# Second layer of a graph network: 15 block products of 512 columns in place of 7 products of 384, with sums moved between engines

## The chip, the cores and the metric

The kernel runs on one core of one Trainium2 chip. The core has a matrix engine (TensorE, PE in the profile, its weight loads shown as PEld), a vector engine (VectorE, DVE), a scalar engine (ScalarE, ACT), a general engine (GpSimd, POOL) and SyncE (SP), which here only issues transfers. Each works through its own list of instructions in order, and they wait for each other by semaphores. The metric is the device time of one execution in microseconds.

## The reference

Two layers run over 128 graphs of 64 nodes with 768 features, so over 8192 rows. In each layer the rows are normalised and clipped at zero (h), and the layer's result is added to its input. The change leaves the first layer's mathematics alone. The second is:

```python
h = jnp.maximum(_layernorm(x, axis=-1), 0.0)
# for each of 6 heads (768 -> 128 columns): hh = h @ W
attn = tanh(hh) @ w_src + swapaxes(tanh(hh) @ w_dst, -1, -2)
attn = softmax(where(adj == 0, -999, leaky_relu(attn, 0.2)))
feat = elu(attn @ hh + b)
gate = sigmoid(h @ H_w.T + H_b)
x = x + gate * feat + (1.0 - gate) * h
```

The heavy part is h times two 768x768 matrices: the six heads side by side (`w_cat`) and the gate (`hw_t`). Everything is float32.

## The kernel before, in words

A tile is 128 rows, that is two graphs; a pair p is two tiles, t0 = 2p and t1 = 2p + 1, and there are 32 pairs. The program has two passes over all pairs.

The first pass (from L289) computes layer 0. Each pair needs 15 block products of a 2x3 by 3x3 scheme, with three weights one after the other in each product (L549, 90 matmuls of 256 columns). `A_SUMS` and `B_SUMS` (L23, L37) are the sums of operand blocks and weight blocks, and `PRODUCTS` (L54) lists each product's operands, its PSUM bank, whether it starts the bank anew, and the output block its bank is added to. `finish` (L571) normalises the pair's result, and stores h in `H1D` and x + h in `XH1`, both in device memory. During the last pair `fetch` (L270) loads and combines the second layer's weights.

The second pass (from L641) computes layer 1. For each pair, `turn` (L704) transposes h through PSUM and makes the operands of a Winograd form of the 2x2 by 2x2 scheme: seven products p1 to p7 (L774 on), each of three matmuls of 384 columns, once for the heads (s = 0) and once for the gate (s = 1). That makes 42 matmuls per pair (L738), in six PSUM banks: three names with two buffers each. `copy` and `add` (L755, L769) take the banks into the tiles HS (heads) and Z (gate).

Then each tile goes through a chain of small steps:
- `heads` (L811): tanh on ScalarE (L814); the product with w_src on GpSimd (L816), summed per head on ScalarE with six accumulating copies (L824); the product with w_dst summed by VectorE (L821); six small GpSimd steps (L825 to L832) split the sums into three bf16 parts.
- `rows` (L840): a matmul turns the sums into rows, which VectorE (L846) and ScalarE (L848) lay out.
- `softmax` (L854): a matmul gives the logits (L860); VectorE keeps those of edges (L862), ScalarE applies the leaky slope (L864), VectorE takes the maximum (L866), ScalarE six exponentials with their sums (L870), VectorE divides (L872, L873).
- `turn_p` and `attend` (L877, L888): transposes of the probabilities and 24 matmuls of 64 rows; VectorE adds the bias (L903). `swap` (L834) fetches the rows of the other graph by a transfer inside the core.
- `final` (L905): an exponential on ScalarE (L911) and four VectorE operations over 768 columns (L912 to L915), then a plain transfer to the output (L916).

The order is written as steps: `main(p)` gives a list of matmul steps, and `merged` (L176) places the side steps of `before` (the next pair's operands) and `behind` (the previous pair's chain) at given step numbers. The build then fixes one list per engine, in which nothing overtakes.

Of the kernel before, what the change touches and what calls it, by code (L numbers as in the profile page):

```python
# [8 lines left out]
F32 = mybir.dt.float32  # L9
# [61 lines left out]

PLACES = ("g6", "g10", "b11", "b21", "g12", "w", "g14", "b01", "b10", "b20", "b02", "b12", "b22",
          "v", "b00")


@with_exitstack
def kernel(
# [24 lines left out]

# [58 lines left out]
    XH1 = [dram.tile([2 * P, D], F32, name=f"xh1_{p}") for p in range(NP)]  # L166
# [30 lines left out]
    nc.vector.memset(mhalf, -0.5)  # L197

# [33 lines left out]

    PL = 3 * KQ * CQ
    BL = KH * HALF
# [5 lines left out]
    def signed(to, s0, x, s1, y):  # L240

        if s0 == "-":
# [4 lines left out]
    NAMES2 = ("11", "21", "T3", "22", "T1", "T2", "T4")  # L247
    bv = {n: [of_weights((2 * i + s) * BL, BL).rearrange("p (k n) -> p k n", k=KH) for s in range(2)]
          for i, n in enumerate(NAMES2)}
    REST = 2 * len(NAMES2) * BL  # L250
    rest = [of_weights(REST + i * D, D) for i in range(9)]
    assert REST + 9 * D <= len(PLACES) * PL

    SUMS2 = {"T1": ("T3", "11"), "T2": ("22", "T1"), "T4": ("21", "T2"), "T3": ("22", "T3")}

    def sum_of_weights(to):
        a, b = SUMS2[to]
        for s, t in enumerate(bv[to]):
            nc.vector.tensor_sub(t, bv[a][s], bv[b][s])
# [10 lines left out]
    def fetch():  # L270

        def blk_of(name, h, q):
            for s, src in enumerate((w_cat, hw_t)):
                nc.sync.dma_start(
                    bv[name][s],
                    src[h * HALF : (h + 1) * HALF, q * HALF : (q + 1) * HALF].rearrange(
                        "(k p) n -> p k n", p=P))

        return [(30, lambda: load_h(0)),
                (13, lambda: blk_of("11", 0, 0)),  # L280
                (20, lambda: blk_of("21", 1, 0)),
                (31, lambda: blk_of("T3", 0, 1)),
                (37, lambda: blk_of("22", 1, 1)),
                (52, lambda: (sum_of_weights("T1"), sum_of_weights("T3"))),
                (57, lambda: sum_of_weights("T2")),
                (68, lambda: sum_of_weights("T4"))]


    with ExitStack() as px:  # L289
# [29 lines left out]
        bw = {n: of_weights(i * PL, PL) for i, n in enumerate(PLACES)}  # L319

# [7 lines left out]
        def form_b(n):  # L328

            s0, x, s1, y, at = B_SUMS[n]  # L330
            if at:
                bw[n] = bw[at]
            tc.keep_in_program_order(signed(bw[n], s0, bw[x], s1, bw[y]))
# [237 lines left out]
        def finish(p):  # L571
            for k in range(2):
                t = 2 * p + k
                to = small.tile([P, 2], F32, name="rn")
                stats(X[t], to)
                h = keep.tile([P, D], F32, name="hf", bufs=2)
                nc.scalar.activation(h, X[t], AF.Relu, scale=to[:, 0:1], bias=to[:, 1:2])
                nc.sync.dma_start(H1D[p][k * P : (k + 1) * P, :], h)
                nc.gpsimd.tensor_add(X[t], X[t], h)
                nc.sync.dma_start(XH1[p][k * P : (k + 1) * P, :], X[t])  # L580
# [60 lines left out]
    with ExitStack() as px:  # L641
# [5 lines left out]
        XH, AI = {}, {}  # L647
# [10 lines left out]
        def load_x(p):  # L658
            for k in range(2):
                t = 2 * p + k  # L660
                XH[t] = work.tile([P, D], F32, name="x", bufs=3)
                nc.sync.dma_start(XH[t], XH1[p][k * P : (k + 1) * P, :])
# [4 lines left out]
        hbb = rest[6]  # L667
        wsd = wb.tile([P, 2, D], F32, name="wsd")
        nc.sync.dma_start(bb, row(b_att, P))
        nc.sync.dma_start(hbb, row(hb, P))  # L670
# [30 lines left out]
        HS, HX, Z, PB = {}, {}, {}, {}  # L701
        A11, A12, A22, S1, S2, S3, S4 = {}, {}, {}, {}, {}, {}, {}

        def turn(p, k, h):  # L704

            ps = pss.tile([P, KH, P], F32, name="ps")
            for i in range(KH):
                kb = h * KH + i
                nc.tensor.transpose(ps[:, i, :], H1[2 * p + k][:, kb * P : (kb + 1) * P], ident)  # L709

            def new(which, name):
                which[p] = work.tile([P, KH, P], F32, name=name)
                return which[p]

            if (k, h) == (0, 0):
                nc.scalar.copy(new(A11, "a11"), ps)
            elif (k, h) == (0, 1):
                nc.scalar.copy(new(A12, "a12"), ps)
            elif (k, h) == (1, 1):
                nc.scalar.copy(new(A22, "a22"), ps)  # L720
            else:
                nc.vector.tensor_sub(new(S3, "s3"), A11[p], ps)
                nc.vector.tensor_add(new(S1, "s1"), A22[p], ps)  # L723
                nc.gpsimd.tensor_sub(new(S2, "s2"), S1[p], A11[p])
                nc.gpsimd.tensor_sub(new(S4, "s4"), A12[p], S2[p])

        def main(p):

            bank = {}
            steps = []  # L730
            t0, t1 = 2 * p, 2 * p + 1

            def mm(b, s, a, w, first):
                for q in range(KH):
                    def step(q=q):
                        if first and q == 0:
                            bank[b, s] = psm.tile([P, 512], F32, name="pm" + ("c" if b == "d" else b))
                        nc.tensor.matmul(bank[b, s][:, :HALF], a[p][:, q, :], bv[w][s][:, q, :],  # L738
                                         start=(first and q == 0), stop=(q == KH - 1),
                                         skip_group_check=True)  # L740
                    steps.append(step)

            def after(step):
                last = steps[-1]
                steps[-1] = lambda: (last(), step())

            def part(t, s, q):
                if s == 0:
                    return HS[t][:, q * HH : (q + 1) * HH, :]
                return Z[t][:, q * HALF : (q + 1) * HALF].rearrange("p (h o) -> p h o", h=HH)  # L750

            def sums(b, s):
                return bank[b, s][:, :HALF].rearrange("p (h o) -> p h o", h=HH)

            def copy(t, s, q, b):  # L755
                def step():
                    if t not in HS:
                        HS[t] = rest[t % 4].rearrange("p (h o) -> p h o", h=H)
                    if s == 1 and t not in Z:
                        Z[t] = work.tile([P, D], F32, name="z", bufs=4)  # L760
                    if s == 0:
                        nc.scalar.copy(part(t, s, q), sums(b, s))
                    else:
                        nc.vector.tensor_add(  # L764
                            part(t, s, q), sums(b, s),
                            hbb[:, q * HALF : (q + 1) * HALF].rearrange("p (h o) -> p h o", h=HH))
                after(step)

            def add(t, s, q, b):  # L769
                def step():  # L770
                    nc.vector.tensor_add(part(t, s, q), sums(b, s), part(t, s, q))
                after(step)

            def p1(s):  # L774
                mm("a", s, A11, "11", True)
                copy(t0, s, 0, "a")

            def p2(s):
                mm("c", s, A12, "21", True)
                add(t0, s, 0, "c")  # L780

            def p5(s):
                mm("b", s, S1, "T1", True)
                copy(t1, s, 1, "b")

            def p6(s):
                mm("a", s, S2, "T2", False)
                copy(t0, s, 1, "a")

            def p4(s):  # L790
                mm("d", s, A22, "T4", True)
                copy(t1, s, 0, "d")

            def p7(s):
                mm("a", s, S3, "T3", False)
                add(t1, s, 0, "a")
                add(t1, s, 1, "a")

            def p3(s):
                mm("b", s, S4, "22", False)  # L800
                add(t0, s, 1, "b")

            order = ((p1, 0), (p2, 0), (p5, 0), (p1, 1), (p6, 0), (p2, 1), (p5, 1), (p4, 0),
                     (p6, 1), (p7, 0), (p4, 1), (p3, 0), (p7, 1), (p3, 1))
            if p == NP - 1:
                order = [(f, s) for s in range(2) for f in (p1, p2, p5, p6, p4, p7, p3)]
            for f, s in order:
                f(s)
            return steps

        def heads(t):  # L811
# [3 lines left out]
            pr = work.tile([P, H, DO], F32, name="pr", bufs=1)  # L815
            nc.gpsimd.tensor_mul(pr, th, wsd[:, 0, :].rearrange("p (h o) -> p h o", h=H))  # L816
            sd = small.tile([P, H], F32, name="sd")
            sg = small.tile([P, 3, H], F32, name="sg")
            for h in range(H):
                no = work.tile([P, DO], F32, name="no", bufs=1)  # L820
# [206 lines left out]
```

## Time and profile before

The time is 2554.71 us, the median of three runs (2554.43 to 2555.62). The profiled execution spans 2552.4 us, with a mean granted TensorE clock of 0.993.

| engine | busy, us | share of the span | instructions |
|---|---|---|---|
| PE | 2501.2 | 98% | 12780 |
| PEld | 1858.1 | 73% | 12780 |
| DVE | 1977.2 | 77% | 4309 |
| ACT | 887.8 | 35% | 2596 |
| POOL | 566.0 | 22% | 863 |

The first pass ends at about 1514 us, where the first transposes of the second pass stand in the time line. A row of the page gives each engine's busy share in 40 slices of 64 us, in tenths (9 is 90% or more). A time line's row gives start, length, engine, line, operation, output<-inputs, shapes, count, and in brackets how long the engine was idle before it and what ended that. A window's row gives the window, its length, and then busy time and count for PE, PEld, DVE, ACT and POOL, the granted clock, the share of the transfer engines and GB/s. Register, branch and semaphore instructions are not counted as busy.

### The profile page before, as it was taken

Reading aid. Unit: us, or ns where it says so; the run is one execution under the profiler, and the core shown is the slowest. Engines: PE = TensorE matmul, PEld = TensorE weight load, DVE = VectorE, ACT = ScalarE, POOL = GpSimd, SP = SyncE. Lnnn points to the kernel's source line nnn. Section 1 sums busy time; section 2 is a strip of 40 time slices with the busy share of each in tenths; the row PEclk is TensorE's granted clock in tenths of the full one; section 3 lists DMA queues with packets and bytes.
Section 4 is the critical chain, followed back from the end, with each engine's and each line's share of the span. In section 5 each row is a group of like instructions: output and inputs, shape, how many; then the busy total and the mean of one; then the engine's idle time right before and its main releaser. Section 6 shows DMA issues by size and latency. Waiting matters only on the chain.

```text
span 2552.4 us, 35949 instructions
## 1 busy us (share of the span) xinstructions
PE 2501.2 (98%) x12780; PEld 1858.1 (73%) x12780; DVE 1977.2 (77%) x4309; ACT 887.8 (35%) x2596; POOL 566.0 (22%) x863
## 2 busy tenths in 40 slices
PE   5999999999999999999999999999999999999996
PEld 4888888888888888888888875656556665656663
DVE  8977677776777777777777446888888888888888
ACT  1221211212212112121121215555555555555555
POOL 0111121111211112111111023333333333333332
PEclk8999999999999999999999999999999999999998
DMA  5112121121111211112111152333333333333332
GB/s 174 44 52 67 40 78 41 41 78 40 67 52 40 79 40 58 60 40 79 40 48 67 38 190 64 102 102 102 102 102 102 102 102 101 102 102 102 101 101 81
DMA packets 104134, 199.06 MB, mean 78 GB/s; under 512 B 35354, under 2 KB 46221, under 8 KB 103954
## 3 DMA queue, kind: packets, MB, share of 16 engines
q1 hardware_dynamic: 103800, 196.70, 24.2%
q8 instruction: 101, 1.65, 0.3%
q14 instruction: 79, 0.65, 0.1%
q10 hardware_dynamic: 154, 0.06, 0.0%
HBM read 95.67 MB, written 75.50 MB: 67 GB/s over the span
## 4 chain that ended last, share of the span: by engine, by line
PE 92%; DVE 3%; DMA 2%; issue 1%; POOL 1%; ACT 1%; SPq 0%; DVEq 0%; POOLq 0%; ACTq 0%
PE pwa L549 19%; PE pwb L549 16%; PE pma L738 14%; PE pmb L738 10%; PE pmc L738 9%; PE pwc L549 6%; PE pwd L549 6%; PE pb L502 5%; PE ps L898 2%; PE ps L709 2%; PE ps L882 1%; PE pwd L533 1%; DVE op L245 1%; DVE weights L245 0%; DMA weights<-in_wself_t_dram 0%
## 5 line engine op out<-in xcount | busy, mean ns | idle before, releaser
L549 PE MATMUL pwa<-weights,op 128*128 128x256 f32 x2304 | 542.8, 383 | 4.1 <-DVE x L541 2.9
L549 PEld LDWEIGHTS pwa<-weights,op 128*128 128x128 f32 x2304 | 423.3, 190 | 73.3 <-DVE x L541 11.7
L510 ACT COPY op<-pb 128x768 f32<-128x768 f32 x160 | 124.1, 797 | 841.4 <-PE pb L502 841.4
L549 PE MATMUL pwb<-weights,op 128*128 128x256 f32 x1536 | 372.5, 383 | 12.6 <-DVE x L543 9.5
L245 DVE TENSOR_TENSOR op<-op 128x768 f32<-128x768 f32 x256 | 238.7, 953 | 154.2 <-ACT op L510 154.1
L549 PEld LDWEIGHTS pwb<-weights,op 128*128 128x128 f32 x1536 | 285.8, 191 | 60.8 <-DVE x L543 10.7
L738 PE MATMUL pmb<-weights,s 128*128 128x384 f32 x768 | 295.1, 494 | 0.5 <-DVE s L723 0.5
L738 PE MATMUL pmc<-weights,a 128*128 128x384 f32 x768 | 285.4, 488 | 0.0
L738 PE MATMUL pma<-weights,s 128*128 128x384 f32 x768 | 279.4, 486 | 0.0
L481 POOL COPY c<-cnt 128x243 bf16<-128x243 bf16 x64 | 46.3, 751 | 721.4 <-PE pb L489 674.3
L738 PEld LDWEIGHTS pmb<-weights,s 128*128 128x128 f32 x768 | 137.6, 190 | 87.1 <-issue 17.3
L738 PEld LDWEIGHTS pma<-weights,s 128*128 128x128 f32 x768 | 140.0, 190 | 80.8 <-DVE z L764 0.2
L738 PEld LDWEIGHTS pmc<-weights,a 128*128 128x128 f32 x768 | 136.5, 190 | 81.9 <-issue 12.3
L816 POOL TENSOR_TENSOR pr<-th,wsd 128x768 f32<-128x768 f32 x64 | 119.5, 1868 | 299.6 <-ACT th L814 236.4
L549 PE MATMUL pwc<-weights,op 128*128 128x256 f32 x768 | 184.9, 383 | 0.0
L219 DVE BATCH_NORM_STATS2 st<-x 128x6 f32<-128x384 f32 x256 | 138.3, 552 | 50.2 <-DMA x<-in_x_dram 48.8
L549 PE MATMUL pwd<-weights,op 128*128 128x256 f32 x768 | 176.2, 379 | 0.0
L226 POOL TENSOR_TENSOR rn<-ve,mhalf 128x1 f32<-128x1 f32 x128 | 70.8, 553 | 470.0 <-DVE ve L225 466.4
L549 PEld LDWEIGHTS pwc<-weights,op 128*128 128x128 f32 x768 | 143.2, 190 | 25.1 <-issue 7.0
L502 PE MATMUL pb<-r,h 64*128 64x192 f32 x1536 | 153.0, 340 | 8.0 <-ACT h L411 7.7
L549 PEld LDWEIGHTS pwd<-weights,op 128*128 128x128 f32 x768 | 145.9, 190 | 19.8
L502 PEld LDWEIGHTS pb<-r,h 64*128 64x128 f32 x1536 | 124.7, 189 | 42.8 <-issue 30.5
(150 smaller groups left out, 3944.4 us busy)
## 6 DMA issues: line engine op xcount, KB each, us to landing
x<-in_x_dram SPq DMA_DIRECT2D x64, 384.0 KB
h<-hf SPq DMA_DIRECT2D x64, 384.0 KB
xh<-x SPq DMA_DIRECT2D x64, 384.0 KB
h<-h SPq DMA_DIRECT2D x64, 384.0 KB
x<-xh SPq DMA_DIRECT2D x64, 384.0 KB
weights<-weights SPq DMA_DIRECT2D x128, 192.0 KB
out_dram<-f SPq DMA_DIRECT2D x62, 384.0 KB
ai<-in_adj_dram SPq DMA_DIRECT2D x64, 64.0 KB
```

The source lines that it names most:

```text
L219: ins = nc.vector.bn_stats(st[:, i, :], src[:, i * HALF : (i + 1) * HALF])
L226: nc.gpsimd.tensor_tensor(to[:, 0:1], ve, mhalf, op=OP.pow)
L245: return (nc.vector.tensor_add if s1 == "+" else nc.vector.tensor_sub)(to, x, y)
L481: nc.gpsimd.tensor_copy(c3, CNT[p][:, k, :, None].to_broadcast([P, NROW, 3]))
L502: nc.tensor.matmul(ps[:, g, i * 3 * N : (i + 1) * 3 * N], H0[t][s, kb * P : (kb + 1) * P], rts[p % 2][s, k].rearrange("p s n -> p (s n)"), ...
L510: nc.scalar.copy(a.rearrange("p h s (g n) -> p g (h s) n", g=GT), ps[:, :, : 6 * N].rearrange("p g (x n) -> p g x n", n=N))
L533: nc.tensor.matmul(bank[b][:, :CQ], CT_T[p, k][: 3 * (e - a), i, :], tabs[i][:, q * CQ : (q + 1) * CQ], start=(first and i == 0), stop=Tru ...
L549: nc.tensor.matmul(bank[b][:, :CQ], OPS[p, an][:, q, s, :], bw[bn][:, (s * KQ + q) * CQ : (s * KQ + q + 1) * CQ], start=(first and q == s ...
L709: nc.tensor.transpose(ps[:, i, :], H1[2 * p + k][:, kb * P : (kb + 1) * P], ident)
L738: nc.tensor.matmul(bank[b, s][:, :HALF], a[p][:, q, :], bv[w][s][:, q, :], start=(first and q == 0), stop=(q == KH - 1), skip_group_check= ...
L816: nc.gpsimd.tensor_mul(pr, th, wsd[:, 0, :].rearrange("p (h o) -> p h o", h=H))
L898: nc.tensor.matmul(po[r][o, c, :], PT[t][s, c, o], (HS if r == g else HX)[t][s, 2 * c + r, :], start=True, stop=True)
```

## The change

The second pass takes over the first pass's 2x3 by 3x3 scheme. h is cut in blocks of 128 rows by 256 columns, each weight in blocks of 256 by 256. The two weights' blocks stand side by side, so that one matmul has 512 columns, the first 256 for the heads and the others for the gate. A product is two such matmuls, and a pair has 15 products, 30 matmuls. For the last pair the products are done for the heads first and then for the gate, with 256 columns. PSUM: two buffers for bank a, one for each of b, c and d, two for everything else.

What moves beside it:
- the operand sums (`form`) are 11 VectorE operations of 256 columns per pair, in place of two VectorE and two GpSimd sums of 384;
- the first addition into an output block is split: ScalarE copies the heads' half, VectorE adds the gate's bias to the other;
- `heads`: one VectorE product of 1536 columns for both w_src and w_dst, and twelve accumulating copies on ScalarE;
- the division of the softmax moves behind the attention: six VectorE operations of 128 columns multiply by the reciprocal sum and add the bias;
- `finish` stores (h + 1)/2 in `HHD` (one more ScalarE operation and transfer), and x + h directly in the output; `final` then needs three VectorE operations, and adds its result to the output by an accumulating transfer issued by GpSimd;
- `heads` of tile t0 starts in the tile's own pair, at step 25 of 30, instead of the next.

The purpose is fewer matmul columns per pair on TensorE, with less work for VectorE and GpSimd around them. The core of the diff:

```diff
 def finish(p):   # first pass
-                nc.sync.dma_start(XH1[p][k * P : (k + 1) * P, :], X[t])
+                nc.sync.dma_start(of[t * P : (t + 1) * P, :], X[t])
+                hh = keep.tile([P, D], F32, name="hh", bufs=1)
+                nc.scalar.activation(hh, h, AF.Identity, scale=0.5, bias=half)
+                nc.sync.dma_start(HHD[p][k * P : (k + 1) * P, :], hh)
...
+        def form(p, *names):
+            for n in names:
+                s0, x, s1, y = A_SUMS[n]
+                t = OPS[p, n] = work.tile([P, KQ, P], F32, name="op", bufs=17)
+                signed(t, s0, OPS[p, x], s1, OPS[p, y])
...
+            def read(b, c, sign, first, ss):
+                k, q = int(c[0]), int(c[1])
+                cols = slice(q * CQ, (q + 1) * CQ)
+                to = hzs[(2 * p + k) % 4][:, ss, cols]
+                ps = bank[b][:, : (ss.stop - ss.start) * CQ].rearrange("p (s n) -> p s n", n=CQ)
+                op = nc.vector.tensor_add if sign == "+" else nc.vector.tensor_sub
+                if not first:
+                    if sign == "+":
+                        op(to, ps, to)
                     else:
+                        op(to, to, ps)
+                    return
+                if ss.start == 0:
+                    nc.scalar.activation(to[:, 0], ps[:, 0], AF.Copy,
+                                         scale=1.0 if sign == "+" else -1.0)
...
+            def product(an, bn, b, first, c, sign, begins, ss):
+                def step(q):
+                    if first and q == 0:
+                        bank[b] = psm.tile([P, 512], F32, name=f"pm{b}", bufs=2 if b == "a" else 1)
+                    n = ss.stop - ss.start
+                    nc.tensor.matmul(
+                        bank[b][:, : n * CQ], OPS[p, an][:, q, :],
+                        bw2[bn][:, (2 * q + ss.start) * CQ : (2 * q + ss.stop) * CQ],
+                        start=(first and q == 0), stop=(q == KQ - 1), skip_group_check=True)
+                    if q == KQ - 1:
+                        read(b, c, sign, begins, ss)
...
 def heads(t):
-            nc.gpsimd.tensor_mul(pr, th, wsd[:, 0, :].rearrange("p (h o) -> p h o", h=H))
+            nc.vector.tensor_mul(pr, th[:, None].to_broadcast([P, 2, H, DO]),
+                                 wsd.rearrange("p s (h o) -> p s h o", h=H))
...
             for h in range(H):
-                nc.vector.scalar_tensor_tensor(no, th[:, h, :], 1.0, wsd[:, 1, h * DO : (h + 1) * DO],
-                                               op0=OP.mult, op1=OP.mult, accum_out=sd[:, h : h + 1])
+                nc.scalar.activation(pr[:, 1, h, :], pr[:, 1, h, :], AF.Copy, accum_out=sd[:, 1, h : h + 1])
...
 def attend(t):
-            for r in range(2):
-                nc.vector.tensor_add(fv[:, r], po[r], bb[:, None, :].to_broadcast([P, HH, DO]))
+            for h in range(H):
+                nc.vector.scalar_tensor_tensor(
+                    FF[t][:, h * DO : (h + 1) * DO], po[h % 2][:, h // 2, :], DN[t][:, h : h + 1], bb,
+                    op0=OP.mult, op1=OP.add)
...
 def final(t, c0=0, c1=D):
-            nc.vector.scalar_tensor_tensor(f, f, -1.0, H1[t][:, c], op0=OP.add, op1=OP.subtract)
+            nc.vector.scalar_tensor_tensor(f, f, 0.5, HM[t][:, c], op0=OP.mult, op1=OP.subtract)
             nc.vector.scalar_tensor_tensor(f, Z[t][:, c], 1.0, f, op0=OP.add, op1=OP.mult)
-            nc.vector.scalar_tensor_tensor(f, f, 0.5, XH[t][:, c], op0=OP.mult, op1=OP.add)
-            nc.sync.dma_start(of[t * P : (t + 1) * P, c], f)
+            nc.gpsimd.dma_start(of[t * P : (t + 1) * P, c], f, accum_op=OP.add)
...
 def behind(p):
-            return [(0, lambda: (heads(t0), swap(t0))),
-                    (3, lambda: (heads(t1), swap(t1))),
-                    (5, lambda: load_x(p)),
-                    (6, lambda: gate(t0)),
-                    (7, lambda: gate(t1)),
-                    (16, lambda: rows(t0)),
-                    (19, lambda: softmax(t0)),
-                    (22, lambda: rows(t1)),
-                    (25, lambda: softmax(t1)),
-                    (31, lambda: turn_p(t0)),
-                    (34, lambda: attend(t0)),
-                    (35, lambda: final(t0)),
+            return [(0, lambda: gate(t0)),
+                    (1, lambda: (heads(t1), swap(t1))),
+                    (2, lambda: load_x(t0)),
+                    (4, lambda: gate(t1)),
+                    (4, lambda: rows(t0)),
+                    (6, lambda: softmax(t0)),
+                    (10, lambda: load_x(t1)),
+                    (11, lambda: rows(t1)),
+                    (13, lambda: softmax(t1)),
+                    (12, lambda: turn_p(t0)),
+                    (14, lambda: attend(t0)),
+                    (15, lambda: final(t0)),
...
```

## The prediction

> **What bounds the kernel now.** I read the page first (shares, slices, chain of waits), then windows, then the time line of the second pass.
>
> ```profile
> PE   5999999999999999999999999999999999999996
> PEld 4888888888888888888888875656556665656663
> DVE  8977677776777777777777446888888888888888
> ...
> PE 92%; DVE 3%; DMA 2%; issue 1%; POOL 1%; ACT 1%; SPq 0%; DVEq 0%; POOLq 0%; ACTq 0%
> ```
>
> TensorE is busy throughout and holds the chain; from slice 24 on (the second pass) VectorE is at eight tenths too. The ends of matmuls are modelled, so I check TensorE by its pace. The window of one pair of tiles, cut between two casts of the same kind (L848):
>
> ```profile
> 1588.98 0.26 ACT L848 CAST lrow<-ps 18x128 bf16<-18x128 f32 x1 [1.40 <-DVE rrow L846]
> ...
> 1620.62 0.26 ACT L848 CAST lrow<-ps 18x128 bf16<-18x128 f32 x1 [1.39 <-DVE rrow L846]
> ```
> ```profile
> 1588.98:1620.62 31.64, 31.64 (x156) 18.98 (x155) 26.69 (x60) 18.38 (x68) 10.35 (x19) 1.00 0.34 102
> ```
>
> A pair takes 31.64 us; the columns are TensorE, weight loads, VectorE, ScalarE, GpSimd. What is a matmul worth? The chain of waits, cut at starts, gives twelve of each width:
>
> ```profile
> 1511.06 2.59 PE pwa L549 x12
> ...
> 1533.46 3.87 PE pma L738 x12
> ```
>
> One f32 matmul is two instructions here (84 of 384 columns per pair for 42 in the code). 256 columns take 0.216 us, 384 take 0.3225: two columns per 1.667 ns and 2.5 ns more. So L738 takes 84 x 0.3225 = 27.1 us of the pair, and 4.55 us are transposes, attention and logits; nothing is left. The second pass is bound by TensorE.
>
> For the other engines I need the distance between instructions, not their busy time:
>
> ```profile
> 1497.70 2.62 DVE L259 TENSOR_TENSOR weights<-weights 128x1152 f32<-128x1152 f32 x2
> ```
> ```profile
> 2001.41 0.33 PE L860 MATMUL ps<-rrow,lrow 82*128 82x384 bf16 x1
> 2001.85 0.58 DVE L862 COPY_PREDICATED a<-ai,ps 128x384 f32<-128x384 int32 x1 [0.32 <-PE ps L860]
> 2002.46 0.52 ACT L864 ACTIVATE al<-a 128x384 f32<-128x384 f32 x1 [1.24 <-DVE a L862]
> ...
> 2009.48 1.02 DVE L771 TENSOR_TENSOR weights<-pma,weights 128x384 f32<-128x384 f32 x2 [0.73 <-PE pma L738]
> ...
> 2018.47 0.29 ACT L824 ACTIVATE pr<-pr 128x128 f32<-128x128 f32 x1
> 2018.76 0.30 ACT L824 ACTIVATE pr<-pr 128x128 f32<-128x128 f32 x1
> ```
>
> Two VectorE operations of 1152 columns span 2.62 us and one lasts 1.36, so the second starts 1.265 after the first; for 384 columns that is 0.47. So a VectorE operation occupies its queue for columns x 1.04 ns + 0.065 us, and a dependent instruction sees it some 0.1 us later. Head sums on ScalarE follow each other by 0.29 us; six exponentials (L870, the same way) take 2.1 us with their sums. A released engine starts 0.03 us after its releaser; VectorE starts 0.44 us after the start of a 384-column logits matmul.
>
> **What the Trainium skill says.** "SBUF — State Buffer", Who interferes with whom: a VectorE instruction with two SBUF inputs contends with a GpSimd instruction that reads SBUF. The trace agrees:
>
> ```profile
> 2016.21 1.92 POOL L816 TENSOR_TENSOR pr<-th,wsd 128x768 f32<-128x768 f32 x1 [7.57 <-ACT th L814]
> 2016.38 2.56 DVE L913 SCALAR_TENSOR_TENSOR f<-f,h 128x768 f32<-128x768 f32 x1
> ...
> 2026.07 0.95 DVE L913 SCALAR_TENSOR_TENSOR f<-f,h 128x768 f32<-128x768 f32 x1
> ```
>
> "TensorE: Matmul & The Clock Gate", Back-to-back issue gap: the isolated gap of a warm matmul is columns/2.4 GHz + 2.5 ns; per pass, that is the pace above. "DMA: Bandwidth & Descriptors", SWDGE vs HWDGE vs iDMA: an accumulating transfer must be issued from GpSimd, whose cores write its descriptors in software. No transfer of the kernel before is of this kind.
>
> **The change, part by part**
>
> *Products.* 30 matmuls of 512 columns replace 42 of 384: 60 passes x (426.7 + 2.5 ns) = 25.75 us instead of 27.1. With the 4.55 us beside them TensorE needs 30.3 us a pair, 1.34 less; over 31 pairs 41 us. This is the possible gain. Transposes and attention stay as many.
>
> *VectorE, per pair, with 1.04 ns and 0.065 us:* 11 sums of activations of 256 columns (0.33 each), 9 reads of 512 (0.60), 6 of 256 (0.33), two head products of 1536 (1.67), 12 attention reads of 128 (0.20), 6 final operations of 768 (0.87), and 2 x 1.7 for rows, mask, maximum and reciprocal as before: 25.5 us. It loses the 2.8 us in which L913 and L915 lay behind L816 in one tile of a pair (2.56 and 2.13 against 0.95 and 1.00), two final operations, the division of the probabilities and the old sums. So VectorE's load hardly moves (26.7 before), against a shorter pair.
>
> *ScalarE:* 24 head sums x 0.29 = 7.0 us instead of 12 x 0.29; some 23 us of busy time in all, not a bound by itself. *GpSimd* loses L816 and the Winograd sums (5.7 us) and gains two issues. For one accumulating issue I bound the price between 0.33 us (SyncE's issue of the same size) and 3 us, and take 1.5: it waits between the head sum and the casts of tile t0, which have 3 us of slack. Landing is needed only when the buffer is reused, about 20 us later.
>
> *The new order.* Each product is added out of its PSUM bank soon after it ends, and bank a (and b) is used again two or three products later: about 3.4 us of slack, against 5 us and six banks before. VectorE's queue is in order and holds long stretches in front of these reads. So I follow the built order once round, from R, the matmul that turns tile t1's head sums into rows. A hop costs 0.03 us:
> - R to the final step of t0: rows to VectorE 0.36 (L862's 0.44 less half the columns), product 0.47, maximum of t0 0.55, four of its six exponentials until its transposes can go and t1's logits follow on TensorE (1.8), 0.44 to the mask, then 0.58 mask, 0.52 leaky, 0.55 maximum, 2.1 exponentials of t1, the reciprocal 0.22, which stands in front of t0's last four attention reads (0.9), 0.94 exponential. With hops 9.6 us.
> - VectorE then runs without a pause: t0's final 3 x 0.87 with three sums 3 x 0.33, two reads 1.2, six attention reads of t1 1.2, head product of t0 1.67, t1's final and three sums 3.6, and last the read of product 13 (0.69), which the next product 1 needs, since it takes that bank. 12.0 us.
> - Product 1 0.15 + 1.72, 0.2 to ScalarE, its copy 0.25, tanh of t1 0.85, head product 1.76, twelve head sums 3.6, five GpSimd steps 1.32 (spacing of L830, L832), 0.2 to the rows matmul, the next R: 10.1 us with hops.
>
> Sum 31.7 us. By TensorE from product 1 on instead of ScalarE and GpSimd: 31.5. Both exceed 30.3, so TensorE waits some 1.2 us a pair, mostly in front of product 1, and the period is 31.7 against 31.64. The gain goes into a loop of waits through VectorE.
>
> *Outside the steady pairs.* First pass: one more activation and transfer per tile; the matmul order is unchanged and VectorE runs 2 us ahead of TensorE where it waits for x, so 0 to 3 us, I take 1. Start of the second pass: twelve transposes through two PSUM buffers and f1 before product 1: 1.5. Pairs 0 and 1 have no loop behind them yet: -2.5. Pairs 2 to 30: 29 x 0.05 = 1.5. Last pair and tail: before, 58 us (2494.5 to 2552.4); after, 38 us of VectorE work (the built order summed by the rule above), 10 of waits and 4.7 for the last transfer (as long as the one in the chain of waits): -5, between -10 and +3. Sum -3.5: **2551 us, no change**.
>
> **Rivals**
> - *TensorE keeps its pace* (0.23): the loop is shorter than I count by 1.3 us. For it: VectorE's load alone (25.5 of 30.3 us) would allow it, and it was at the same share before without a stall. Against it: every term above is measured. 2551 - 29 x 1.3 = 2513, about 2511 with pair 1.
> - *Slower* (0.27): hops add up, the attention reads with a pointer operand cost more than 0.20 us (ten are in the loop), or an accumulating issue holds GpSimd beyond 3 us, so that the rows of t0 come late. A pair of 32.4 us: 2551 + 29 x 0.7 = 2571. Against it: no such operation is seen to be dear before.
> - *No change* (0.50), as above.
>
> **How the numbers follow.** The forecast case has 2551 with a spread of some 9 us (0.3 us a pair); the bounds for "same" are 2549.6 and 2559.8. So of its 0.50 I give 0.20 to faster, 0.20 to within, 0.10 to slower. Faster 0.20 + 0.23 = 0.43; same 0.20 and 0.02 of the slower rival's edge = 0.22; slower 0.35. The range takes in the first rival and half of the second: 2508 to 2578.
>
> **What would show it.** Right: the rows casts of one tile lie 31.7 us apart; the first matmuls on bank a wait about 1 us per pair for VectorE's subtraction (L738 of the new code); the rows matmul waits for GpSimd; VectorE near 26 us a pair; the final operations all near 0.95 us. Wrong: casts 30.3 us apart and TensorE without waits (first rival); L861 spaced at 0.28 us or GpSimd's issues over 3 us (second). A first pass later than 1514 us by more than 5 us would be another error.

## The result, and the profile after

The changed kernel takes 2579.5 us (median of four runs, 2578.7 to 2580.8) beside 2554.6 us for the kernel before (2554.2 to 2555.6): a ratio of 1.0097, 95% interval 1.008 to 1.0115. It is 25 us slower. The forecast was 2551 us, no change, and its range ended at 2578.

Line numbers from here on are those of the changed kernel. L755 is a product's matmul; L736, L738, L746 and L748 are VectorE's reads of the product banks, L741 ScalarE's; L241 and L243 are the operand sums. L774 is the tanh of a tile, L776 its head product, L781 and L783 its head sums; L784, L789 and L791 are GpSimd's small steps, of which L789 makes the bf16 casts. L803 is the rows matmul, L807 the cast behind it, L831 the reciprocal, L861 an attention read, L871 to L875 the final operations with the output's issue.

First the page of the kernel after: three rows of the slices and the shares of the chain of waits.

```profile
PE   5999999999999999999999999999999999999996
PEld 4788888888888888888888864444444444444444
DVE  8977777777777777777777557888888888888887
...
PE 71%; DVE 18%; ACT 6%; issue 4%; DMA 1%; POOL 1%; SPq 0%; POOLq 0%; DVEq 0%; ACTq 0%
```

The slices of PE still show nines everywhere. The chain tells more: TensorE's share of it fell from 92% to 71%, and VectorE's rose from 3% to 18%. The work that sets the end now runs through VectorE. The time line gives the period, between the same cast in two neighbouring pairs:

```profile
2010.61 0.26 ACT L807 CAST lrow<-ps 18x128 bf16<-18x128 f32 x1
...
2042.87 0.26 ACT L807 CAST lrow<-ps 18x128 bf16<-18x128 f32 x1
```
```profile
2010.61:2042.87 32.26, 31.25 (x131) 14.13 (x130) 26.58 (x54) 22.51 (x96) 7.45 (x16) 1.00 0.42 100
```

A pair takes 32.26 us, against some 31.65 before and the 31.7 of the forecast; TensorE's granted clock, the first of the last three columns, is full (1.00) in the steady pairs of both kernels. VectorE is busy for 26.58 us of it (forecast: near 26). The waits of TensorE over 1560 to 2530 us show one wait per pair (total us, how often, longest), and the time line shows it beside the loop that causes it:

```profile
PE pma L755 <- DVE weights L738: 29.3, 29, 1.0
```
```profile
2021.69 0.96 DVE L872 SCALAR_TENSOR_TENSOR f<-e,f 128x768 f32<-128x768 f32 x1 [0.41 <-ACT e L871]
...
2026.51 1.63 DVE L861 SCALAR_TENSOR_TENSOR f<-ps,dn,bb 128x128 f32<-128x128 f32 x6
...
2034.07 1.12 PE L755 MATMUL pma<-weights,op 128*128 128x512 f32 x2 [1.01 <-DVE weights L738]
```

This is the wait that the prediction described, in size and cause, and the loop is there. Going round it from R (2012.09 in this pair): to t0's final step at 2021.69 are 9.60 us (forecast 9.6); to the waiting matmul at 2034.07 are 12.38 (12.0); to the next R at 2044.35 are 10.28 (10.1). The end of the last leg:

```profile
2044.10 0.20 POOL L789 CAST sdb<-sg 128x18 bf16<-128x18 f32 x1
```
```profile
2043.36 1.02 PE L755 MATMUL pma<-weights,op 128*128 128x512 f32 x2
2044.35 0.28 PE L803 MATMUL ps<-idr,sdb 128*82 128x192 bf16 x1
```

R starts 0.05 us after GpSimd's last cast has ended, and so it does in every steady pair. It follows the matmul in front of it by 0.56 us, where the rows matmul of t0, whose casts are done earlier, follows by 0.43. So R waits 0.13 us for GpSimd. No list of waits has this, since idle time counts from the modelled end of the matmul before. The last leg runs through ScalarE and GpSimd, as forecast, and TensorE's own work is only 0.13 us shorter.

The row of L861 holds the mis-sized term: six attention reads in 1.63 us, the last 0.34 long, so (1.63 - 0.34) / 5 = 0.258 us apart. The prediction took 0.20. Ten of them lie in the loop: 0.58 us a pair.

By stage, from the two traces (2577.0 and 2552.4 us long), cut at the first transposes of the second pass and at the first matmul of a pair's product 1:

| stage | forecast, us | measured, us |
|---|---|---|
| first pass | +1 | -0.2 |
| start of the second pass, to product 1 | +1.5 | +0.6 |
| pairs 0 and 1 | -2.5 | +1.0 |
| pairs 2 to 30 | +1.5 | +17.9 |
| last pair and tail | -5 | +5.4 |

The steady pairs hold most of the miss (29 x 0.61 = 17.7), and the two ends of the second pass the rest. The end of the first pass lies anywhere from 1513.6 to 1515.2 us in the runs below, so its -0.2 means nothing.

### The profile page after: what moved, and what is told of

It reads as the page before. It is cut to its first block, busy times and chain, and to the rows that moved or that the text cites. A ratio compares the mean times of both kernels' runs of the same rounds, so it can differ in the third digit from the quotient of the medians.

```text
span 2577.0 us, 35545 instructions
## 1 busy us (share of the span) xinstructions
PE 2489.3 (97%) x12072; PEld 1714.2 (67%) x12072; DVE 1980.3 (77%) x4130; ACT 1079.5 (42%) x3588; POOL 492.3 (19%) x801
## 4 chain that ended last, share of the span: by engine, by line
PE 71%; DVE 18%; ACT 6%; issue 4%; DMA 1%; POOL 1%; SPq 0%; POOLq 0%; DVEq 0%; ACTq 0%
PE pwa L544 19%; PE pwb L544 16%; PE pwc L544 6%; PE pma L755 6%; PE pwd L544 6%; PE pmb L755 6%; PE pb L497 5%; DVE f L861 3%; ACT pb L829 3%; DVE op L243 3%; PE pmc L755 2%; DVE pr L776 2%; DVE f L874 2%; DVE f L872 2%; DVE weights L738 1%
## 5 line engine op out<-in xcount | busy, mean ns | idle before, releaser
L243 DVE TENSOR_TENSOR op<-op 128x768 f32<-128x768 f32 (+1 forms) x512 | 339.8, 683 | 156.4 <-ACT op L505 154.5
L755 PE MATMUL pma<-weights,op 128*128 128x512 f32 (+1 forms) x792 | 381.5, 597 | 35.2 <-DVE weights L738 29.3
L755 PE MATMUL pmb<-weights,op 128*128 128x512 f32 (+1 forms) x528 | 252.4, 591 | 3.6 <-DVE weights L738 3.5
L755 PEld LDWEIGHTS pma<-weights,op 128*128 128x128 f32 x792 | 137.8, 191 | 173.8 <-issue 96.4
L225 POOL TENSOR_TENSOR rn<-ve,mhalf 128x1 f32<-128x1 f32 x128 | 89.0, 695 | 530.5 <-DVE ve L224 526.9
L755 PEld LDWEIGHTS pmb<-weights,op 128*128 128x128 f32 x528 | 97.0, 193 | 118.4 <-issue 82.9
L572 ACT ACTIVATE hf<-x,rn 128x768 f32<-128x768 f32 x64 | 65.8, 1028 | 213.7 <-DVE rn L226 213.7
L829 ACT ACTIVATE pb<-al,mx 128x64 f32<-128x64 f32 x384 | 128.3, 335 | 14.8 <-DVE mx L825 14.8
L574 POOL TENSOR_TENSOR x<-x,hf 128x768 f32<-128x768 f32 x64 | 115.9, 1812 | 85.4 <-ACT hf L572 85.4
```

The costliest lines, as they stand in the source:

```text
L225: nc.gpsimd.tensor_tensor(to[:, 0:1], ve, mhalf, op=OP.pow)
L243: return (nc.vector.tensor_add if s1 == "+" else nc.vector.tensor_sub)(to, x, y)
L755: nc.tensor.matmul(bank[b][:, : n * CQ], OPS[p, an][:, q, :], bw2[bn][:, (2 * q + ss.start) * CQ : (2 * q + ss.stop) * CQ], start=(first a ...
L829: nc.scalar.activation(pb[:, h, :], al[:, h, :], AF.Exp, bias=mx[:, h : h + 1], accum_out=dn[:, h : h + 1])
```

## The experiments

The theory after the result: the loop through VectorE sets the pair, and the pointer operand's extra time is what the forecast lacked. The rivals: GpSimd sets it, held up by its accumulating issues, or held up by VectorE. Where an edit below changes the order of one engine only, all other engines keep the changed kernel's order.

**The pointer operand.** The division is left out and a fixed number takes its place:

```diff
-FF[t][:, h * DO : (h + 1) * DO], po[h % 2][:, h // 2, :], DN[t][:, h : h + 1], bb,
+FF[t][:, h * DO : (h + 1) * DO], po[h % 2][:, h // 2, :], 0.015625, bb,
```

> Order of every engine as in the changed kernel; the six attention reads of a tile (L861) multiply by the fixed number 1/64 and no longer by a value per row taken from a tile, so the division of the softmax is left out. If the pointer is what makes these reads 0.26 us apart and not the 0.20 us that 128 columns were reckoned at, they fall to 0.20 us; ten of them are in the loop of waits: 0.6 us less a pair, period 31.7, as reckoned beforehand, 2561 us. If the 0.26 us have another cause, or if the reads are not in the loop: 32.26, 2579 us.

Its time line:

```profile
2000.23 0.26 ACT L807 CAST lrow<-ps 18x128 bf16<-18x128 f32 x1
...
2015.89 1.27 DVE L861 SCALAR_TENSOR_TENSOR f<-ps,bb 128x128 f32<-128x128 f32 x6
...
2031.89 0.26 ACT L807 CAST lrow<-ps 18x128 bf16<-18x128 f32 x1
```

The casts are 31.66 us apart, six reads take 1.27 us and so lie 0.20 apart: what the prediction had assumed gives the pair that the prediction had computed. The whole takes 2559.7 us (1.0019 of before, 1.0012 to 1.0026), 20 less than the changed kernel. That this one operand is the cause of the longer pair is shown.

**Is the loop where the prediction drew it?** VectorE does t1's reciprocal behind t0's last four attention reads, not in front of them:

```diff
 VectorE:
-L831 (t1)
 L861 x4 (t0)
+L831 (t1)
```

> Same instructions as the changed kernel, and the same order on every engine, but for one thing: in each pair the reciprocal of tile t1 (L831) stands behind t0's last four attention reads (L861) on VectorE and no longer in front of them. Loop of waits: t0's reads end 0.87 us earlier, so its exponential and all that VectorE does behind it come earlier; period 32.26 - 0.87 = 31.4 us or a little less (31.1, if the wait at the end of the loop shrinks as well), 29 pairs: 2545 to 2554 us. VectorE's amount of work as the bound: nothing is taken away, period 32.26, 2579 us. GpSimd (its issues of the accumulating transfers) as the bound: 2579 us.

Measured: 2557.7 us (1.0011, 1.0004 to 1.0017). Steady pairs take 31.56 us, 0.70 less. Its time line and TensorE's waits:

```profile
2007.10 1.64 DVE L861 SCALAR_TENSOR_TENSOR f<-ps,dn,bb 128x128 f32<-128x128 f32 x6 [0.19 <-PE ps L857]
2008.65 0.18 DVE L831 RECIPROCAL dn<-dn 128x6 f32<-128x6 f32 x1
```
```profile
PE pma L755 <- DVE weights L738: 10.5, 29, 0.8
```

The six reads now lie in one run, and TensorE's waits fall from 29.3 to 10.5 us. The loop does pass through this place. It gained less than the 0.87 to 1.16 expected, and the trace shows where the difference went. From R (2001.00) to t0's final step (2009.74) are 8.74 us, 0.86 less than in the changed kernel. But VectorE's run is now 12.54 us and no longer without a pause: the first operand sum (L243) waits for ScalarE's copy of the next pair's transposes, and starts 1.03 us after L872 instead of 0.88.

**The other end of the VectorE leg.** The reads of products 13 and 14 go ahead of t1's final operations, so that the waiting matmul is released sooner:

```diff
 VectorE:
-L776, L872, L243, L873, L243, L874, L243, L738, L736
+L776, L738, L736, L872, L243, L873, L243, L874, L243
```

> Same instructions as the changed kernel; on VectorE the reads of products 13 and 14 (L738, L736) stand in front of t1's final operations (L872 to L874 with their three sums) and no longer behind them, so TensorE's wait of 1.0 us in front of the last product on bank a should go. Loop of waits through VectorE's queue: VectorE has as much in front of t1's head product as before, and only its pauses there go (0.22 and 0.1 us, and 0.1 more), so 0.3 to 0.45 us a pair: period 31.8 to 31.95, 2566 to 2571 us. TensorE's wait for the bank as the cost by itself: 1.0 us a pair, period 31.25, 2549 us. VectorE's amount of work as the bound: 2579 us.

It missed on the wrong side: 2630.0 us (1.0299, 1.0285 to 1.0313), with pairs that take 33.2 or, more often, about 34.9 us. The time line of GpSimd, VectorE and TensorE there:

```profile
2023.54 3.16 POOL L784 TENSOR_TENSOR sg<-sd,gm 128x12 f32<-128x12 f32 x1 [5.61 <-ACT pr L781]
2026.56 0.41 DVE L746 TENSOR_TENSOR weights<-pma,weights 128x256 f32<-128x256 f32 x1
2026.65 0.87 POOL L875 DMA_DIRECT2D out_dram<-f  x1
2028.67 1.72 POOL L791 TENSOR_TENSOR sg<-sg,sdb 128x18 f32<-128x18 f32 x1
2030.70 0.28 PE L803 MATMUL ps<-idr,sdb 128*82 128x192 bf16 x1 [2.53 <-POOL sdb L789]
```

L784 works on 12 columns and takes 0.21 us elsewhere; here it takes 3.16. VectorE ran L243, L873, L243, L874, L243 and L241 without a pause meanwhile, all with both inputs in SBUF, and L784 ended when L746 began, which reads PSUM. "SBUF — State Buffer", Who interferes with whom, in the Trainium skill says that the two engines share a port pair under an exclusive lock, and that a VectorE instruction with two SBUF inputs contends with a GpSimd instruction that reads SBUF. The trace agrees on the operands, and shows more than the page says: not one instruction but a run of six held the small one. The rows of t0 then come late, and TensorE waits 70.7 us in 28 pairs for L789.

The pair of 33.2 us is 0.95 longer than in the changed kernel, and the 1.7 us beyond it in the longer pairs have a second cause. Behind the wait the granted clock falls to half (0.50 in this window), and the next product, four instructions in the trace, takes 3.60 us where such a product takes 1.88 to 1.98 at full clock:

```profile
2030.90:2034.30 3.40, 3.40 (x6) 1.32 (x6) 0.88 (x2) 3.36 (x23) 0.38 (x2) 0.50 0.31 87
```
```profile
2030.82 3.60 PE L755 MATMUL pma<-weights,op 128*128 128x512 f32 x4
```

From R to R, every longer pair holds one such stretch of 3.4 us and no pair of 33.2 does. Between 1560 and 2530 us there are 16 of them, so about 27 of the 50 us that this run takes more than the changed kernel belong to the clock. In the steady pairs of the changed kernel, where TensorE waits 1.0 us, there are none.

The rival reading is that the accumulating issue, which stands in GpSimd's queue, is the cause. The same order with the output written by a plain transfer (f alone, x + h left out):

```diff
-nc.gpsimd.dma_start(of[t * P : (t + 1) * P, c], f, accum_op=OP.add)
+nc.sync.dma_start(of[t * P : (t + 1) * P, c], f)
```

> The order of the run in which the reads of products 13 and 14 came first (period 33.2 and 34.9 by turns, 2630 us), but the output is f alone, by a plain transfer from SyncE, so GpSimd has only the head-sum steps; the sum with x + h is left out. If the accumulating issue between t0's head sum (L784) and its casts (L789) made that run slow, it goes: period 31.8 to 31.95, 2562 to 2570 us. If GpSimd's small steps wait for an end of VectorE's run of operations with two SBUF inputs (L784 took 3.16 us there, 0.21 us elsewhere), they still do: L784 at 3 us, only the 0.6 to 0.9 us of the issue go, period 32.5 to 34, 2590 to 2620 us.

2627.3 us (1.0284, 1.027 to 1.0298), and L784 still took 3.17 us. With no accumulating issue the loss stays; that rival falls for this order as the sole cause. The issue does cost something: at full clock a pair takes 32.93 us, 0.28 less, within what was expected. This trace has 20 stretches at half clock and not 16, and they take the gain back. Then the test of the port: a VectorE read of PSUM between two operations of the run, just behind the start of L784:

```diff
 VectorE:
-L776, L738, L736, L872, L243, L873, L243, L874, L243
+L776, L738, L872, L243, L873, L736, L243, L874, L243
```

> As the slow run with the reads of products 13 and 14 in front of t1's final operations (2630 us), but the read of product 14 (L736, one input in PSUM) stands between the second and the third part of the final operations. If GpSimd's small steps get through only where VectorE turns from operations with two SBUF inputs to one that reads PSUM, L784 ends at that read: about 0.7 us and not 3.16, the casts come in time and the loss goes: period 31.8 to 32.3, 2566 to 2582 us. If the lateness of t0's rows there has another cause (the reads themselves, the transfers), 33 to 35 us a pair as before, 2610 to 2630 us.

```profile
2020.78 0.95 DVE L873 SCALAR_TENSOR_TENSOR f<-f,x 128x768 f32<-128x768 f32 x1
2021.10 0.69 POOL L784 TENSOR_TENSOR sg<-sd,gm 128x12 f32<-128x12 f32 x1 [5.61 <-ACT pr L781]
2021.64 0.68 DVE L736 TENSOR_TENSOR weights<-pmb,weights 128x512 f32<-128x512 f32 x1
2023.83 0.88 POOL L875 DMA_DIRECT2D out_dram<-f  x1 [2.04 <-DVE f L874]
```

L784 takes 0.69 us and ends as L736 begins: that the read frees it is shown. The time, though, did not fall (2631.2 us; 1.0299, 1.0283 to 1.0314), and the half-clock stretches are 16 again. GpSimd's next instruction is t1's accumulating issue, which now waits 2.04 us for VectorE's L874, and t0's casts stand behind it; then L789 and L791 are held for 1.17 and 1.72 us more. So freeing L784 only brings the next obstacles to light, and the rows of t0 are as late as before. No run takes these away as well.

**Both moves of VectorE's order.** The reciprocal's move and the reads of products 13 and 14 in front:

> Both changes of order together (the reciprocal of t1 behind t0's reads; the reads of products 13 and 14 in front of t1's final operations), no instruction more or less. Loop of waits: both gains add, 1.2 to 1.6 us a pair, period 30.65 to 31.05, close to TensorE's own 30.3; 2533 to 2545 us, faster than the kernel before (2554.6). Amount of work on VectorE, or GpSimd, as the bound: 2579 us.

2546.0 us (0.9965, 0.9952 to 0.9979), with steady pairs of 31.09 us: a microsecond above the expected span of times, and faster than before. L784 took 0.43 us there and the three casts 0.50, 0.27 and 0.20, though the operations beside L784 (L243 and L873) both have two inputs in SBUF. So a read of PSUM is one way for GpSimd to get its turn, and not the only one. The issue waited 2.3 us for L874 here too, and the rows of t0 came in time, so that wait alone does not make them late. With read 14 between L873 and L874 instead, as in the last run but one:

> The same shift of the read of product 14 in the run with both changes of order (31.09 us a pair, 2546 us), where L784 took 0.43 us. GpSimd's steps were not late there in the steady pairs, so 31.0 to 31.1 us a pair; the first pairs, which were 35.0, 36.2 and 32.1 us apart, should lose their 3 to 8 us: 2538 to 2546 us. If the shift itself costs (the next product on bank b waits for the read), above 2546 us.

Missed: 2586.0 us (1.0119, 1.0102 to 1.0135). L784 took 0.69 us, but the issue waited 2.04, and L789 and L791 took 1.17 and 1.71; TensorE waited 54.7 us for L789, about 1.9 in a pair, and the steady pairs kept the full clock. Why GpSimd gets its turn in one of these orders and not in the other, with nearly the same VectorE operations beside it, is not settled.

**Does GpSimd limit the changed kernel itself?** There too its steps of t0 are stretched, as its time line shows for t0 and then t1:

```profile
2031.86 1.62 POOL L784 TENSOR_TENSOR sg<-sd,gm 128x12 f32<-128x12 f32 x1 [5.61 <-ACT pr L781]
...
2041.17 0.21 POOL L784 TENSOR_TENSOR sg<-sd,gm 128x12 f32<-128x12 f32 x1 [4.54 <-ACT pr L781]
```

To shorten the last leg, the head sums of t1 with w_src were taken off ScalarE:

```diff
+if t % 2:
+    nc.vector.tensor_reduce(sg[:, 2, :], pr[:, 0], AX.X, OP.add)
+else:
     for h in range(H):
         nc.scalar.activation(pr[:, 0, h, :], pr[:, 0, h, :], AF.Copy, accum_out=sg[:, 2, h : h + 1])
```

> Undoes half of one part of the change: for tile t1 the products with w_src are summed by one VectorE reduction (768 columns, 0.87 us) and no longer by six copies on ScalarE (1.76 us); t0 as in the changed kernel; the build orders the rest anew. Loop of waits: 1.76 - 0.87 = 0.9 us less a pair on the way from t1's tanh to its rows, period 31.4, 2553 us. VectorE's amount of work as the bound: 0.87 more a pair, period 33.1, 2605 us. GpSimd's steps held up by VectorE: t1's five steps now meet VectorE operations where they had an idle VectorE, which can take back all of the gain: 32.3, 2580 us.

2574.6 us (1.0081, 1.0065 to 1.0096), with a shorter and a longer pair by turns, 31.97 us on average: of the expected 0.9 a pair, 0.3 came. TensorE's wait for L738 fell to 6.1 us, and a wait of 25.9 us for the cast of L789 took its place. The expectation also overlooked that in the changed kernel's order the last leg could give no more than 0.13 us, since TensorE's own work lies just behind. In the changed kernel GpSimd's stretched steps of t0 use up slack only: the last cast ends 0.98 us before the rows matmul of t0. The steps of t1 are not stretched, and TensorE's 0.13 us of waiting for them are above.

**The accumulating output alone.** The same plain transfer as above, in the changed kernel's order:

> Order as in the changed kernel on TensorE, VectorE, ScalarE and GpSimd, but the second pass writes f alone, by a plain transfer that SyncE issues; the sum with x + h is left out. Loop of waits: the issues of 0.9 us on GpSimd lie beside the loop, period stays 32.26; at the end of the program the last transfer takes some 3.5 us after the last VectorE operation, as before the change, and not the 7.9 us of the accumulating one: 2575 us. Accumulating issues as the cause of the loss: they also hold VectorE's operands and the casts on GpSimd; period down by 0.5 us or more, 2560 us or less.

2571.9 us (1.0072, 1.0058 to 1.0086). The period is 32.26 as before the edit, so the issues cost the steady pairs of this order nothing. The gain lies at the ends. The first pair's cast comes 2.35 us earlier: TensorE's wait there is 2.7 us instead of 3.4, and a stretch at half clock that follows it in the changed kernel's trace is missing. And the span ends 3.1 us after the last VectorE operation instead of 8.5.

**The ends.** For the last two tiles x + h is loaded early, added by VectorE and written by a plain transfer; the last `finish` of the first pass gets a later step, and so does the +1 on the bias:

```diff
+nc.vector.tensor_add(f, f, XO[t][:, c])
+nc.sync.dma_start(of[t * P : (t + 1) * P, c], f)   # last two tiles only
...
-more = [(3, lambda: finish(NP - 1))] if p == 0 else []
+more = [(24, lambda: finish(NP - 1))] if p == 0 else []
```

> The changed kernel with the ends of the second pass changed alone: the last finish of the first pass at step 24, the bias's +1 at step 26, and the last two tiles adding x + h from a load and leaving by plain transfers. The period stays 32.26. The wait of 3.4 us in the first pair should go, and the end come some 4 us earlier: 2571 to 2574 us; 2579 if both are hidden elsewhere.

2574.4 us (1.0082, 1.0065 to 1.0098), 5.1 less than the changed kernel. The tail behind the last VectorE operation falls from 8.5 to 2.8 us. At the start the first pair's wait is still 2.9 us: the order that was built had put the bias and the last `finish` early again, and a later step number did not move them.

**A better order by step numbers.** The reciprocal moves to the start of `attend`, t0's transposes one step later, t1's final three:

```diff
-nc.vector.reciprocal(dn, dn)            # softmax
+nc.vector.reciprocal(DN[t], DN[t])      # start of attend
-(12, lambda: turn_p(t0)),
+(13, lambda: turn_p(t0)),
-(22, lambda: final(t1))]
+(25, lambda: final(t1))]
```

> The same work as the changed kernel; the reciprocal of t1 is put behind t0's transposes and attention matmuls, and two step numbers are later (t0's transposes 12 to 13, t1's final operations 22 to 25), so that the operands of the next pair and the reads of the products are no longer behind the final operations. Loop of waits: it becomes shorter than TensorE's own pace, which by the pauseless stretches of these runs is 30.6 to 30.8 us a pair, period 30.7 to 31.0: 2530 to 2541 us. VectorE's amount of work as the bound: 2579 us.

2542.8 us (0.9952, 0.9939 to 0.9964), pairs alternately of 30.8 and 31.5, on average 31.1: two microseconds above the expected span of times, and faster than before. With the edit of the ends beside it:

> As the run with the later step numbers, and the ends of the second pass changed: the last pair of the first pass is finished at step 24 of the second pass's first pair and not at step 3, the bias's +1 (L668, which waits for its load) moves to step 26, and the last two tiles add x + h from a load and leave by plain transfers. If the 3.4 us wait in the first pair comes from what stood in front of the reads on VectorE, 3 us go; if the accumulating transfer's 7.9 us at the end is its own price, 4 us go: 6 to 7 us less than the run without, 2524 to 2534 us. If neither: the same as that run.

2539.7 us (0.9937, 0.9924 to 0.9949): 15 us faster than the kernel before, 40 faster than the changed one. It is 3 us faster than the run ahead of it, where 6 to 7 were expected. The tail gave more than the 4 us expected of it: the span ends 2.8 us after the last VectorE operation, where the run ahead needs 8.8. The first pair's wait fell only from 3.4 to 2.1 us. The profiled executions differ by 7.0 us and the medians by 3.0, so how much the ends are worth in all stays open.

## Why the prediction was wrong

*The loop of waits: right in kind.* The period comes from R, the softmax, a pauseless run of VectorE and TensorE's way back to R, and TensorE waits 1.0 us in it, and 0.13 for GpSimd's cast. The legs were off by 0.0, 0.4 and 0.2 us. The first holds four of the dearer reads and still came out as forecast, so something else in it was counted 0.2 too long; the last was counted 0.2 too short. That these two cancel is luck. The name of the waiting matmul was wrong: bank a collects a pair's products, and only product 1 starts it, so what waits for the read of product 13 is the same pair's last product into that bank, not "the next product 1". The wait and its cause are the same.

*"six attention reads of t1 1.2" and "t0's last four attention reads (0.9)": the step that failed.* Measured at 0.258 us apart, they take 1.55 and 1.03. The 0.20 came from the rule for VectorE, which had been fitted to operations without a pointer operand. The prediction did name this cost, as its rival's ("cost more than 0.20 us (ten are in the loop)"), and named 0.28 as its sign; but it gave that rival 0.27 and the range only half of it. The pair was 0.56 us longer than forecast, and the term is 10 x 0.058 = 0.58. With the operand gone, the pair is 31.66 against 31.7, a match that rests in part on the two errors of 0.2 that cancel.

*"Last pair and tail -5": failed, by 10 us.* The forecast had 38 us of VectorE work, 10 of waits and 4.7 for the last transfer. Measured, from the start of the last pair:

```profile
2513.90:2577.00 63.10, 39.89 (x241) 28.51 (x239) 45.39 (x100) 38.41 (x176) 14.63 (x33) 0.84 0.38 74
```

VectorE is busy for 45.4 us of this and its last operation ends at 2568.4, so it waits 9.2: the waits were right, and the work was 7.4 short. The rule for VectorE gives some 41 us for the operations of this stretch (an estimate, summed over their columns), so that part of the 38 was miscounted before any price came in; which operations were left out is not known.

The end of an accumulating transfer was costed at 4.7 us, as the old plain one; from the last VectorE operation to the end of the span it takes 8.5, against 3.0 before. The time lines of the last operations, after and before:

```profile
2568.27 1.75 POOL L875 DMA_DIRECT2D out_dram<-f  x2 [1.48 <-DVE f L874]
```
```profile
2548.39 1.02 DVE L915 SCALAR_TENSOR_TENSOR f<-f,x 128x384 f32<-128x384 f32 x2
```

After, the issues end at 2570.0, the last transfer lands at 2573.45, 4.6 us after its issue began, and the span ends 3.5 us later. In the run with plain transfers the last one lands 1.9 us after its issue began and the span ends 1.1 later. "DMA: Bandwidth & Descriptors", Latency and other measured facts, in the Trainium skill gives about 1 us to the first byte for a transfer whose descriptors software writes, and 0.6 for the other kind; an estimate from it explains 0.4 of the 2.7 us by which the two landings differ. Behind the landing the changed kernel's trace has a closing instruction of GpSimd (a DRAIN) that ends at 2576.2 only, 2.7 us after the landing; why it takes so long is not shown.

*"Pairs 0 and 1 -2.5": failed, by 3.5.* They have no loop behind them, but the first pair has a wait that was not foreseen:

```profile
1524.79 0.70 PE L755 MATMUL pma<-weights,op 128*128 128x512 f32 x1 [3.39 <-DVE weights L746]
```

VectorE reads this bank late: ahead in its queue stand the last `finish` of the first pass, where it waits 2.77 us for GpSimd, and the bias, whose load it waits 1.7 us for. Behind this wait the clock is at half from 1526.0 to 1529.4, which costs 1.7 us more; in the kernel before it is full there. The stretch does not follow in every execution: with the reciprocal moved it is missing behind a wait of 3.26 us.

*"TensorE needs 30.3 us a pair": a little low.* The shortest steady pairs of any run take 30.8, by turns with longer ones. In the changed kernel TensorE is busy for 31.25 us; part of that is waiting too short to be listed, as R's 0.13, and how much in all is open.

*Right:* VectorE's load, final operations near 0.95 us, GpSimd's slack (an issue takes 0.88 us, assumed 1.5), a first pass that does not come later. "The rows matmul waits for GpSimd" came true for t1, by 0.13 us a pair.

## What to carry over

When an engine's run without a pause lies on a loop of waits, each price in it counts as often as it occurs: ten reads that were 0.06 us dearer cost this kernel most of its 25 us. Price a form of instruction that the trace before does not have from both sides, and put the upper end into the sum where it occurs often. Look at the granted clock where TensorE waits: in one run here, waits of 2.5 us a pair brought stretches at half clock that cost as much again. And follow a loop before taking the change for bad: the same products in another order are 0.5% faster than the kernel before, and 0.6% with the ends changed too.

## What the runs showed of the hardware

- A pointer operand of one value per partition adds 0.06 us to a VectorE operation of 128 columns from PSUM (0.258 against 0.20 apart).
- Back-to-back VectorE operations with two SBUF inputs can hold a 0.21 us GpSimd operation for 3.16 us; one PSUM read among them frees it (0.69 us). In one order it got through without such a read (0.43 us).
- In the three runs where TensorE waited 2.2 to 2.5 us in nearly every steady pair, the clock fell to half at the end of 16 to 20 of these waits, for 3.4 us each time, and the pair took 1.7 us more. Waits of 1.9 us a pair left the steady pairs at the full clock.
- With an accumulating transfer last, the program ends 8.5 us after the last VectorE operation, with a plain one 2.8 to 3.1. In the steady pairs of the changed kernel's order it costs no time.
